# The last score packs of a head group's two sequences, run together in column tiles

## The chip, the cores and the metric

One Trainium2 chip, one core. The kernel computes two layers of a small model in float32. The metric is the time of one execution on the device, in microseconds (us). The changed kernel is run beside this one.

## The reference

Input x has 16 sequences of 256 tokens and 256 features. Each of the two layers is x + s * g on the normalised x, where s is a mixer and g a gate. The change touches the mixer of the second layer, an attention with 16 heads and latent keys:

```python
scores = jnp.einsum('bqhd,bkhd->bhqk', q, k) * scale
scores = jnp.where(mask, scores, jnp.finfo(scores.dtype).min)   # causal
attn = jax.nn.softmax(scores, axis=-1)
out = jnp.einsum('bhqk,bkhd->bqhd', attn, v).reshape(B, S, N_HEADS * V_DIM)
return out @ Wo
```

The first layer (a recurrence and a feed-forward gate) is not touched.

## The kernel before

**Tiling.** Tokens come in 8 chunks of two sequences (512 tokens). Heads come in groups of G = 4, so a chunk has four head groups, and there are 32 groups in all. One group of one sequence is a *unit*; there are 64, numbered i, and the main loop (`for i in range(LAST)`, L1649) spends one *slot* on each. Even slots hold sequence 0 of a group, odd slots sequence 1. Within a chunk the slot has a number r from 0 to 7; slot 31 is r = 7 of chunk 3, slot 34 r = 2 of chunk 4.

**Scores in blocks.** The 256 queries of a sequence are cut into NQ = 8 blocks of 32. Block a, with the four heads stacked, fills 128 rows and sees 32(a + 1) keys. `score_pack` (L1365) multiplies a few blocks into one PSUM bank: pack 0 has blocks 7 and 6, pack 1 has 5, 4 and 3, pack 2 has 2, 1 and 0 (96, 64 and 32 keys). For every block of a pack VectorE adds the mask (one instruction for the pack) and takes the row maximum; ScalarE takes the exponential, into the unit's buffer `pr`, with the row sums in `sr`. There are three PSUM banks for packs and two `pr` buffers, one for even and one for odd units.

**Column tiles.** A product can use the 128x128 array whole (128*128 in the profile) or half of its columns (128*64), so that two products with 64 rows of output stand side by side. Pack 2 of an even unit runs in two halves where it follows the products of values, which run in 64*64 tiles; this holds from slot 6 on. All other packs use the whole array.

**After the exponentials.** `normalise` (L1401) takes a reciprocal of the sums on VectorE and multiplies each block on GpSimd, one instruction for a block. Then three VectorE transposes (`turn`, L1414) write `turned`; the third, z = 0, reads blocks 0 to 3 and needs pack 2. `send` (L1426) stores it to DRAM (`far`) with four DMAs, and `fetch` (L1440) brings it back as `pT`, once for each half of the keys (y) and each sequence (b). `values_of` (L1486) multiplies `pT` by the values (`av`) for both sequences of a group, in the even slot four slots behind the group's first; it uses the half y = 0 first.

**Queries.** For a group two ahead, the odd slot multiplies queries (`pq`), rotates them on VectorE (`qmul`) and GpSimd (`qrot`, `query_rot`, L424); the next even slot begins with `query_move` (L430), eight DMAs that move `qrot` into `qg`.

**Order.** Every engine runs in the order written (`InOrder`), SyncE's DMA queue too: an instruction that waits holds up all behind it. SyncE's order is, in an even slot, query moves, fetch (y = 0, b = 0), the store of the odd unit before, fetch (y = 1, b = 0); in an odd slot, both fetches for b = 1, the store of the even unit before.

Before the change, an even slot's pack 2 comes after the values, then `normalise` of packs 0 and 1; an odd slot's pack 2 stands between the second and third query product, again followed by `normalise` of packs 0 and 1. Pack 2 of either unit is normalised in the slot behind, after that slot's pack 0.

**Other work in the slots.** At r = 6 the router of the next chunk (`router_chunk`, L318): products `pm`, then some twenty small VectorE instructions. At r = 7, in chunks 1 to 6, `fast_begin` (L1589): GpSimd multiplies and adds an output of the chunk before and stores it (`out_dram<-x`), between the normalising of the even unit's pack 2 and of the odd unit's packs 0 and 1. In the last chunk TensorE has output products instead of new queries.

Of the kernel before, what the change touches and what calls it, by code (L numbers as in the profile page):

```python
# [41 lines left out]
def tile_two_layers(ctx: ExitStack, tc: tile.TileContext, d: dict, out: bass.AP):  # L42
    nc = tc.nc

    class InOrder:


        def __init__(self, engine):
            self.engine, self.last = engine, None
# [151 lines left out]
    def bc(ap, n):  # L201

        return ap.unsqueeze(1).to_broadcast([ap.shape[0], n, ap.shape[1]])
# [226 lines left out]
    def query_move(n):  # L430
        q = groups[n]
        for r in range(2):
            for h in range(G):
                sp.dma_start(
                    q.qg[64 + 32 * r : 96 + 32 * r, :, h, :],
                    q.rot[32 * h : 32 * h + 32, r, :].rearrange("p (a q) -> p a q", q=32),
                )


    with ExitStack() as l0:  # L440
# [106 lines left out]
        def tiny(name, n=1):  # L547
            return w0.tile([P, n], F32, tag=name, name=name)
# [43 lines left out]
        u = tiny("u")  # L592
# [127 lines left out]
        def recur_mm(ch, xnT, ring):  # L720
            pb = ring.tile([P, S], F32, tag="mm", name=f"pb_{ch}")
            for c in range(2):
                for b in range(2):
                    pe.matmul(
                        pb[64 * b : 64 * b + 64, :], bT[:, c, :],
                        xnT[:, c, b * S : (b + 1) * S], start=(c == 0), stop=(c == 1),
                    )
            return pb

        def recur_in(ch, pb):  # L730

            v = a2.tile([P, S], F32, tag="v", name=f"v_{ch}")
            w = a2.tile([P, S], F32, tag="w", name=f"w_{ch}")
            v0.tensor_tensor(v, pb, ct, ALU.mult)
            swapped(w, pb)
            return v, w
# [519 lines left out]
        v, w = recur_in(ch, recur_mm(ch, xnT, ps_mm))  # L1256
# [73 lines left out]
    def gate_end(ch, jp):  # L1330
        k = chunks[ch]
        g = k.g2[:, 2 * jp : 2 * jp + 2, :]
        ve.scalar_tensor_tensor(g, g, 1.0, k.h, ALU.add, ALU.mult)
# [15 lines left out]
    for t in prs:  # L1349
        for a in range(NQ):  # L1350
            w = 32 * (a + 1)
# [3 lines left out]
    class Unit:  # L1355


        def __init__(self, i):
            self.i = i
            self.ch, r = divmod(i, 2 * NG)  # L1360
            self.g, self.b = divmod(r, 2)
            self.n = f"{self.ch}_{self.g}_{self.b}"
            self.pr = prs[i % NPR]

    def score_pack(u, pi):  # L1365
        k, b, pack = chunks[u.ch], u.b, PACK[pi]
        if pi == 0:
            u.nm = sm1.tile([P, NQ], F32, tag="nm", name=f"nm_{u.n}", bufs=3)
            u.sr = sm1.tile([P, NQ], F32, tag="sr", name=f"sr_{u.n}", bufs=3)
        qg = groups[u.i // 2].qg  # L1370
        sc = ps_sc.tile([P, CH], F32, tag="sc", name=f"sc_{u.n}_{pi}")
        halves = 2 if pi == 2 and u.b == 0 and u.i > 4 else 1
        m = P // halves
        for a, o in pack:
            w = qg[:, b * NQ + a, :, :].rearrange("p h q -> p (h q)")
            for y in range(halves):
                pe.matmul(
                    sc[m * y : m * y + m, o : o + 32 * (a + 1)], w[:, m * y : m * y + m],
                    k.kT[:, b * S : b * S + 32 * (a + 1)], start=True, stop=True,
                )  # L1380
        ends = [o + 32 * (a + 1) for a, o in pack]
        step = ends[1] - ends[0]
        n = len(pack)
        assert ends == [ends[0] + step * z for z in range(n)]
        if ends[0] - 32 + step * n <= CH:
            diag = sc[:, ends[0] - 32 : ends[0] - 32 + step * n].rearrange("p (n s) -> p n s", n=n)[:, :, 0:32]
        else:
            diag = sc[:, ends[0] - step : ends[-1]].rearrange("p (n s) -> p n s", n=n)[:, :, step - 32 : step]
        ve.tensor_tensor(diag, diag, bc(kmask, n), ALU.add)
        for a, o in pack:  # L1390
            ve.tensor_reduce(
                u.nm[:, a : a + 1], sc[:, o : o + 32 * (a + 1)], AX.X, ALU.max, negate=True
            )
        for a, o in pack:
            w = 32 * (a + 1)
            ac.activation(
                u.pr[:, OFF[a] : OFF[a] + w], sc[:, o : o + w], AF.Exp,
                bias=u.nm[:, a : a + 1], accum_out=u.sr[:, a : a + 1],
            )

    def normalise(u, packs):  # L1401
        blocks = [a for pi in packs for a, _ in PACK[pi]]
        lo, hi = min(blocks), max(blocks) + 1
        ve.reciprocal(u.sr[:, lo:hi], u.sr[:, lo:hi])
        for a in blocks:
            v = u.pr[:, OFF[a] : OFF[a] + 32 * (a + 1)]
            gp.tensor_scalar(v, v, u.sr[:, a : a + 1], 1.0, ALU.mult, ALU.mult)
# [32 lines left out]
    def fetch(n, y, b):  # L1440

        q = groups[n]
        if y == b == 0:
            q.pT = {}
        if b == 0:
            q.pT[y] = pp.tile([P, G, 3 * P], F32, tag="pT", name=f"pT_{n}_{y}", bufs=3)
        sp.dma_start(
            q.pT[y][64 * b : 64 * b + 64].rearrange("p h q -> p (h q)"),
            q.far[b].rearrange("(y k) s h z q -> y (k s) (h z q)", y=2)[y],
        )  # L1450
# [197 lines left out]
    units = [Unit(i) for i in range(LAST)]  # L1648
    for i in range(LAST):  # L1649
        ch, r = divmod(i, PER)  # L1650
        odd = i % 2 == 1
        u, w = units[i], units[i - 1] if i else None
        here = w is not None and w.i >= LAST - 2
        n = (i + 3) // 2 if odd else (i + 2) // 2
        n = n if n < len(groups) else None
        more = ch + 1 < NCH
        last = ch - 1 if ch == NCH - 1 and r in FINISH else None
        fast = ch - 1 if 0 < ch < NCH - 1 else None

        if not odd and n is not None:  # L1660
            query_move(n)
        if odd and i > 2:
            fetch((i - 3) // 2, 0, 1)
            fetch((i - 3) // 2, 1, 1)
        elif i and not odd:
            fetch((i - 2) // 2, 0, 0)
        score_pack(u, 0)
        if w:
            normalise(w, (2,))
        if fast is not None and r > 3:  # L1670
            fast_begin(fast, r)
        if ch > 1 and r == 0:
            fast_begin(ch - 2, 0)
        out_weights(i)
        if r == 1:
            gate_end(ch, 0)
        if r == 2:
            gate_end(ch, 1)
            if more and ch:
                norm_end(ch + 1)  # L1680
        if r == 5 and more:
            kv_end(ch + 1)
        if i == LAST - 1:

            finish_mm(last, 3, 0, NPAIR)
            finish_out(last, 3)
            last = None
        if w:
            for z in (1, 2):
                turn_here(w, z) if here else turn(w, z)  # L1690

        if r == 0:
            mid_chunk(ch)
        if r == 7 and more:
            key_chunk(ch + 1)
        if n is not None:
            query_mm(n, 0 if odd else 3)
            if not odd:
                query_lat(n, 3)
        if i == 5:  # L1700
            values_of(0)
        score_pack(u, 1)

        if odd and n is not None:
            query_mm(n, 1)
            query_mul(n, 0)
        if w:
            if here:
                turn_here(w, 0)
            else:  # L1710
                turn(w, 0)
                send(w)
        if not odd:
            if i > 4:
                values_of((i - 4) // 2)
            if i:
                fetch((i - 2) // 2, 1, 0)
        score_pack(u, 2)
        normalise(u, (0, 1))

        if odd and n is not None:
            query_mm(n, 2)
            query_mul(n, 1)
            query_rot(n)
            query_lat(n, 2)
        if r < 2:
            gate_begin(ch, r)
        if r == 0 and more and ch:
            norm_begin(ch + 1)
        if r == 2 and more:  # L1730
            transpose_chunk(ch + 1)
        if r == 4 and more:
            kv_begin(ch + 1)
        if r == 6 and more:
            router_chunk(ch + 1)
        if last is not None:
            j = FINISH.index(r)
            finish_mm(last, j, 0, NPAIR)
            finish_out(last, j)
        if fast is not None and r in FINISH:  # L1740
            fast_end(fast, r)
# [1 line left out]

    ch = NCH - 1
    u0, u1 = units[LAST - 2], units[LAST - 1]
    normalise(u1, (2,))

    finish_mm(ch, 0, 0, 4)
    finish_mm(ch, 1, 0, 4)
# [86 lines left out]
```

## Time and profile before

| | |
|---|---|
| median of 3 runs | 905.32 us (902.85 to 906.59) |
| profiled execution | 908.37 us, of it the span 906.6 us |
| granted TensorE clock, mean | 0.998 |
| second layer's slots | from about 272 us to the end |
| far<-turned, issue to landing, median | 4.3 us |
| pT<-far, issue to landing, median | 4.9 us |

A line of a timeline gives the start, the duration, the engine, the operation with output<-input, the shape, the count of instructions, and in brackets the idle time before it with what ended it. PE is TensorE, DVE VectorE, ACT ScalarE, POOL GpSimd, SPq SyncE's queue. A float32 product is recorded as two matmuls. L53 is the line of the helper that records the order, so groups are told apart by their tiles.

### The profile page before, as it was taken

Reading aid. Unit: us, or ns where it says so; the run is one execution under the profiler, and the core shown is the slowest. Engines: PE = TensorE matmul, PEld = TensorE weight load, DVE = VectorE, ACT = ScalarE, POOL = GpSimd, SP = SyncE. Lnnn points to the kernel's source line nnn. Section 1 sums busy time; section 2 is a strip of 40 time slices with the busy share of each in tenths; the row PEclk is TensorE's granted clock in tenths of the full one; section 3 lists DMA queues with packets and bytes.
Section 4 is the critical chain, followed back from the end, with each engine's and each line's share of the span. In section 5 each row is a group of like instructions: output and inputs, shape, how many; then the busy total and the mean of one; then the engine's idle time right before and its main releaser. Section 6 shows DMA issues by size and latency. Waiting matters only on the chain.

```text
span 906.6 us, 17800 instructions
## 1 busy us (share of the span) xinstructions
PE 893.3 (99%) x5600; PEld 668.2 (74%) x5600; DVE 666.4 (74%) x2017; ACT 476.1 (53%) x1562; POOL 571.5 (63%) x885
## 2 busy tenths in 40 slices
PE   8999999999999999999999999999999999999997
PEld 7768899888767656677677677667767766777775
DVE  6885687665586879768967876896786688687652
ACT  3334556564436656545554665565466556546451
POOL 1218787878345537687586768748776775876540
PEclk9999999999999999999999999999999999999999
DMA  9730000000013887877887888788788778968881
GB/s 283 236 108 10 1 2 1 1 1 1 1 24 71 195 218 190 217 175 176 212 212 175 211 197 181 177 224 202 175 212 186 198 172 213 221 163 206 198 230 38
DMA packets 197405, 134.02 MB, mean 148 GB/s; under 512 B 143104, under 2 KB 187968, under 8 KB 197312
## 3 DMA queue, kind: packets, MB, share of 16 engines
q1 hardware_dynamic: 195184, 128.69, 57.5%
q0 software_dynamic: 1152, 3.67, 1.3%
q8 instruction: 45, 0.74, 0.4%
q10 hardware_dynamic: 976, 0.53, 0.2%
q14 instruction: 48, 0.39, 0.1%
HBM read 63.11 MB, written 52.95 MB: 128 GB/s over the span
## 4 chain that ended last, share of the span: by engine, by line
PE 89%; DMA 4%; DVE 4%; POOL 1%; SPq 1%; issue 0%; ACT 0%; DVEq 0%; POOLq 0%; ACTq 0%
PE pq L53 21%; PE sc L53 13%; PE po L53 10%; PE av L53 8%; PE r L53 7%; PE f L53 7%; PE ph L53 5%; PE pf L53 5%; PE pg L53 4%; DMA far<-turned 2%; PE pm L53 2%; DMA pT<-far 2%; PE tp L53 2%; PE pkv L53 2%; PE py L53 1%; PE pb L53 1%
## 5 line engine op out<-in xcount | busy, mean ns | idle before, releaser
L53 POOL TENSOR_SCALAR pr<-pr,sr 128x256 f32<-128x256 f32 (+7 forms) x512 | 192.6, 395 | 186.4 <-DVE sr L53 177.6
L53 ACT ACTIVATE pr<-sc,nm 128x256 f32<-128x256 f32 (+7 forms) x512 | 190.2, 382 | 216.0 <-DVE sr L53 138.4
L53 PEld LDWEIGHTS sc<-kT,qg 128*128 128x128 f32 (+1 forms) x1198 | 150.0, 175 | 54.5 <-issue 41.2
L53 PE MATMUL sc<-kT,qg 128*128 128x32 f32 (+6 forms) x1198 | 167.8, 288 | 0.0
L53 DVE TENSOR_REDUCE nm<-sc 128x1 f32<-128x256 f32 (+7 forms) x512 | 127.7, 301 | 6.6
L53 DVE STREAM_TRANSPOSE turned<-pr 128x512 f32<-128x512 f32 x186 | 123.3, 688 | 11.1 <-POOL pr L53 10.9
L53 PE MATMUL pq<-xnT,wlat 128*128 128x512 f32 x256 | 122.6, 602 | 0.0
L53 PE MATMUL pq<-xnT,wrope 128*128 128x512 f32 x256 | 120.2, 593 | 0.0
L53 ACT ACTIVATION_READ_ACCUMULATOR pr<-sc,nm 128x1 f32 x512 | 104.0, 203 | 0.0
L53 PE MATMUL av<-pT,rowv 64*64 64x512 f32 (+2 forms) x992 | 82.4, 443 | 5.3 <-DMA pT<-far 5.3
L53 POOL TENSOR_TENSOR qrot<-qmul,qmul 128x512 f32<-128x512 f32 x64 | 83.6, 1326 | 2.8 <-DVE qmul L53 2.8
L53 DVE TENSOR_TENSOR sc<-sc,kmask 128x96 f32<-128x96 f32 (+1 forms) x192 | 45.5, 237 | 51.6 <-PE sc L53 50.2
L53 DVE TENSOR_TENSOR qmul<-pq,rot_q 128x512 f32<-128x512 f32 x128 | 80.9, 674 | 0.1
L53 ACT ACTIVATE qg<-pq 64x512 f32<-64x512 f32 x128 | 75.5, 590 | 4.3 <-PE pq L53 3.5
L53 PEld LDWEIGHTS av<-pT,rowv 64*64 64x64 f32 x992 | 40.3, 134 | 44.5 <-issue 25.3
L53 PEld LDWEIGHTS pq<-xnT,wrope 128*128 128x128 f32 x256 | 45.7, 191 | 32.4 <-issue 32.1
L53 PEld LDWEIGHTS pq<-xnT,wlat 128*128 128x128 f32 x256 | 45.7, 191 | 31.6 <-issue 31.6
L53 PEld LDWEIGHTS po<-wout,attT 128*128 128x128 f32 x416 | 58.4, 191 | 9.4 <-issue 4.0
L53 PE MATMUL po<-wout,attT 128*128 128x128 f32 (+1 forms) x416 | 64.2, 308 | 0.0
L53 POOL TENSOR_TENSOR rs<-ve,mhalf 128x4 f32<-128x4 f32 (+1 forms) x17 | 16.8, 987 | 48.0 <-DVE ve L53 33.0
L53 PE MATMUL ph<-xnT,p1T 128*128 128x256 f32 (+1 forms) x128 | 44.9, 508 | 0.8 <-DVE xnT L53 0.8
L53 POOL TENSOR_TENSOR attT<-attT,attT 128x512 f32<-128x512 f32 x36 | 45.1, 1272 | 0.0
(229 smaller groups left out, 1522.0 us busy)
## 6 DMA issues: line engine op xcount, KB each, us to landing
far<-turned SPq DMA_DIRECT2D x248, 192.0 KB, 4.3
pT<-far SPq DMA_DIRECT2D x124, 384.0 KB, 4.9
qg<-qrot SPq DMA_DIRECT2D x256, 64.0 KB, 2.5
x<-in_x_dram SPq DMA_DIRECT2D x7, 512.0 KB, 9.5
out_dram<-x POOLq DMA_DIRECT2D x12, 256.0 KB, 3.6
wqn_wo<-in_wq_nopeT_dram SPq DMA_DIRECT2D x4, 512.0 KB, 5.1
wqn_wo<-in_Wo_dram SPq DMA_DIRECT2D x4, 512.0 KB, 5.9
p2T<-in_proj2T_dram SPq DMA_DIRECT2D x2, 512.0 KB, 7.7
```

The source lines that it names most:

```text
L53: r = getattr(self.engine, name)(*args, **kw)
```

## The change

Pack 2 of both units of a group now runs in the even slot, one behind the other, always in two halves of 128*64, behind the products of values (in slots 0, 2 and 4, which have no values, behind pack 1). The odd slot has no pack 2 any more. The odd unit is normalised whole, eight blocks at once, at the place where packs 0 and 1 were; the slot behind an odd slot therefore has no `normalise` at its start. The even unit's `normalise` stays as it was: packs 0 and 1 in its own slot, behind both packs 2, and pack 2 in the odd slot behind.

```diff
     def score_pack(u, pi):
         k, b, pack = chunks[u.ch], u.b, PACK[pi]
-        if pi == 0:
+        if u.nm is None:
             u.nm = sm1.tile([P, NQ], F32, tag="nm", name=f"nm_{u.n}", bufs=3)
             u.sr = sm1.tile([P, NQ], F32, tag="sr", name=f"sr_{u.n}", bufs=3)
...
-        halves = 2 if pi == 2 and u.b == 0 and u.i > 4 else 1
+        halves = 2 if pi == 2 else 1
...
         score_pack(u, 0)
-        if w:
+        if odd:
             normalise(w, (2,))
...
-        score_pack(u, 2)
-        normalise(u, (0, 1))
+        if odd:
+            normalise(u, (0, 1, 2))
+        else:
+            score_pack(u, 2)
+            score_pack(units[i + 1], 2)
+            normalise(u, (0, 1))
...
     u0, u1 = units[LAST - 2], units[LAST - 1]
-    normalise(u1, (2,))
```

More of the change, by code (lines that the diff above doesn't have):

```diff
@@ L1363, in __init__ @@
             self.pr = prs[i % NPR]
+            self.nm = None
     def score_pack(u, pi):
         k, b, pack = chunks[u.ch], u.b, PACK[pi]
-        if pi == 0:
+        if u.nm is None:
             u.nm = sm1.tile([P, NQ], F32, tag="nm", name=f"nm_{u.n}", bufs=3)
```

## The prediction

> **What bounds the kernel now.** First the page: busy time by engine and the chain that ended last.
>
> ```profile
> PE 893.3 (99%) x5600; PEld 668.2 (74%) x5600; DVE 666.4 (74%) x2017; ACT 476.1 (53%) x1562; POOL 571.5 (63%) x885
> PE 89%; DMA 4%; DVE 4%; POOL 1%; SPq 1%; issue 0%; ACT 0%; DVEq 0%; POOLq 0%; ACTq 0%
> ```
>
> TensorE never rests. But a busy TensorE only says that other chains are not longer; one may be just as long. So next, TensorE's waits from 430 to 880 us:
>
> ```profile
> PE av L53 <- DMA pT<-far: 1.8, 2, 1.6
> ```
>
> The one thing it ever waits for is the transposed softmax coming back from DRAM. I follow that path once, from slot 30 (r = 6 of chunk 3) to slot 34. TensorE's timeline:
>
> ```profile
> 563.49 0.59 PE L53 MATMUL sc<-kT,qg 128*64 128x96 f32 x12
> 564.01 2.12 PE L53 MATMUL pm<-wmid,xnT 128*128 128x136 f32 x16
> ...
> 571.47 0.75 PE L53 MATMUL sc<-kT,qg 128*128 128x96 f32 x6
> 572.06 1.96 PE L53 MATMUL pq<-xnT,wlat 128*128 128x512 f32 x4
> ...
> 576.89 1.88 PE L53 MATMUL pq<-xnT,wlat 128*128 128x512 f32 x4
> ...
> 598.52 2.41 PE L53 MATMUL av<-pT,rowv 64*64 64x512 f32 x32
> ```
>
> VectorE waits for the router's products (pm), works through the router without a pause, and only then reaches slot 31's scores, 5.5 us late:
>
> ```profile
> 566.17 0.17 DVE L53 TENSOR_TENSOR lg<-pm,rb_bc 128x16 f32<-128x16 f32 x1 [0.75 <-PE pm L53]
> ...
> 571.45 0.23 DVE L53 TENSOR_TENSOR sc<-sc,kmask 128x64 f32<-128x64 f32 x1
> ...
> 572.35 0.17 DVE L53 RECIPROCAL sr<-sr 128x3 f32<-128x3 f32 x1
> ...
> 575.79 0.70 DVE L53 STREAM_TRANSPOSE turned<-pr 128x512 f32<-128x512 f32 x1
> ...
> 577.09 0.18 DVE L53 RECIPROCAL sr<-sr 128x5 f32<-128x5 f32 x1
> ```
>
> That reciprocal of 572.35 releases GpSimd, which then runs solidly up to the rotated queries (qrot):
>
> ```profile
> 572.68 0.91 POOL L53 TENSOR_SCALAR pr<-pr,sr 128x96 f32<-128x96 f32 x3 [5.32 <-DVE sr L53]
> ...
> 576.46 0.78 POOL L53 DMA_DIRECT2D out_dram<-x  x1 [0.30 <-POOL x L53]
> 577.38 2.03 POOL L53 TENSOR_SCALAR pr<-pr,sr 128x256 f32<-128x256 f32 x5
> 579.38 2.50 POOL L53 TENSOR_TENSOR qrot<-qmul,qmul 128x512 f32<-128x512 f32 x2
> 581.87 0.89 POOL L53 TENSOR_SCALAR pr<-pr,sr 128x96 f32<-128x96 f32 x3
> ```
>
> SyncE's queue stands at its eight query moves until the first qrot is done (idle 578.3 to 580.7), then issues without a pause of its own making (its only holds are landings of its own writes); the last two fetches follow in the second fence:
>
> ```profile
> 580.68 5.37 SPq L53 DMA_DIRECT2D qg<-qrot  x8
> 586.09 0.99 SPq L53 DMA_DIRECT2D pT<-far  x1
> 587.18 2.69 SPq L53 DMA_DIRECT2D far<-turned  x4
> 589.97 4.96 SPq L53 DMA_DIRECT2D pT<-far  x3
> ```
> ```profile
> L53 SPq DMA_DIRECT2D pT<-far x2: 451/520/588, 593.8 to 594.3; - x2
> DMA to landing us min/median/max: 4.4/4.9/5.5
> ```
>
> 594.3 + 5.5 = 599.8: the last block lands then. Slot 34's values begin at 598.52 and reach that block 1.34 us later, at 599.87. The slack is 0.05 us. So there are two bounds of equal length: TensorE, and the chain pm, router, reciprocal, GpSimd, qrot, SyncE, fetch. The same slack at the other chunk ends, landing against use: 443.1/442.7, 520.9/521.5, 678.3/678.2, 757.4/756.7, 835.9/835.8, that is -0.4, 0.7, 0, -0.7, -0.1. The groups between have up to 7 us, or hang on the same SyncE run as the one before.
>
> **The change, part by part.** (1) TensorE loses the odd slot's pack: 571.47 to 572.06, 0.59 us, once per group. (2) It gains a second tiled pack in the even slot. No row shows one alone. Above: 0.52 us (563.49 to 564.01), which includes entering and leaving the mode. Below: pure streaming; four pq instructions take 1.72 us in the timeline (576.89 to the next group at 578.61, a score pack), 0.84 ns per column, and a pack streams 2 x 192 columns with its two halves side by side, 0.32 us. I take 0.34, near the lower end, since the array is in the mode already. Net -0.25 per group for 29 groups, and about -0.2 for groups 0 to 2, whose first pack turns tiled as well, with a switch of mode (0.59 + 0.59 to 0.52 + 0.34, less about 0.1 for entering from the full array). Sum on TensorE: -7.9 us, were it the only bound.
>
> (3) Three normalisations move ahead of qrot on GpSimd. In slot 31 they stood behind it (581.87); start to next start, 0.86 us. What hides it? In slots with r = 1 and 3 SyncE is still busy when qrot ends (slot 33: ready at 597.4, issued at 598.4). At r = 5 the queue does wait, but the fetches it leads to have 5 us of slack. At r = 7 nothing hides it. The reciprocal now stands right behind the transpose that ends at 576.50, and slot 31's exponentials ended by 576.0, so it can come 0.6 us sooner; but GpSimd's store issue ends at 577.24, so normalising starts only 0.09 sooner. Chain: +0.86 - 0.09 = +0.77.
>
> (4) The second tiled pack stands ahead of pm: +0.34 in slot 30, and the router follows pm one for one. VectorE's four extra instructions there (0.7 us, by the first pack's) fit into its waits for pm (0.23 and 0.75). Chain from slot 30's start: +1.11.
>
> (5) ScalarE's three exponentials move with the pack; at 53% it has room, and slot 31's come after a 1.25 us gap anyway. The odd unit's even-slot transposes can start sooner, but its stores queue behind the query moves, so nothing arrives sooner. The probability buffer is free by then: the last transpose that reads it stands earlier on VectorE. One reciprocal per group (0.17 us) vanishes under other work.
>
> TensorE meanwhile comes to slot 34's values 0.34 - 0.59 + 0.34 - 0.59 = -0.49 earlier than before. It will wait about 1.11 + 0.49 - 0.05 = 1.55 us there. From values to values a chunk then changes by 1.11 - 0.49 = +0.62, less what slack there was.
>
> Sum: at the start of the layer, slot 1's qrot leads an unbroken SyncE run to the first waits. Slot 0 gains 0.36 us on TensorE, the reciprocal moves from 287.18 to 286.9, qrot +0.86: +0.58. Chunk 0's end (slot 7, no store there): the reciprocal now follows the transpose that ends at 340.88 instead of waiting until 341.47, so even with pm's +0.34 it comes 0.33 sooner; with the three operations, +0.53, on fetches that TensorE already waits for. Six chunk ends: 6 x 0.62 - 0.72 of positive slack = +3.0. After slot 55 SyncE runs unbroken to the last fetch, and TensorE already waits 1.8 us at 867 and 1.3 us at 885 for it, so later savings vanish and nothing comes back. Total +4.1 us: 908.37 to 912.5 for the profiled execution. That one ran 3.05 us over the median of the runs; carried over, 905.32 + 4.1 = 909.4 us.
>
> [...] The row: inside the tiled pack twelve weight loads fit into 0.52 us, switching included. [...]
>
> **Rivals.** *Faster: TensorE decides.* If fetches arrive early enough, parts 1 and 2 count in full: -7.9 us, 897.4; with half of the chunk ends hidden, about 902. For it: TensorE's 99%; and executions without profiling are 3 us shorter, perhaps in these very transfers. It decides where a chunk end has over 1.6 us of slack. Against it: the rows show 0.7 at most, five times of six none.
>
> *Slower still: the even unit gets late.* The even slot's reciprocal now stands behind the second pack on VectorE (0.7 us), so GpSimd's normalising, the next slot's transposes and the even unit's store follow later. If that store becomes what SyncE stands at, 0.7 us for seven chunks are added, +4.9: 914.3. It decides if the store is ready after the queue reaches it. Against it: slot 32's last transpose ends at 593.3 in slot 33 and the queue reaches its store at 595.0, so 1.7 us are spare.
>
> *The change doesn't do what it says: tiles run one by one.* Then the second pack costs 0.59, TensorE gains nothing, and pm comes 0.25 later in seven chunks: +1.8, 911.2.
>
> **How the numbers follow.** Forecast 0.60, faster 0.20, late even unit 0.13, tiles in turn 0.07. A measurement of this kernel can tell about 0.5%, 4.5 us, from no change, so 909.85 parts same from slower. The forecast's own range is 906.5 to 912.5 (0.15 us either way on seven steps, and each chain varies by some 0.4 us between chunks); two fifths of it are over the line. Slower: 0.24 + 0.13 + 0.06 = 0.43. Faster by over 0.5%: two thirds of its rival, 0.13. Same: 0.36 + 0.07 + 0.01 = 0.44. The range 901 to 914.5 leaves out the lower half of the faster rival and the upper half of the late one.
>
> **What would show it.** Right: TensorE's waits for pT between 430 and 880 grow several-fold, at the r = 2 slot behind each chunk end; eight normalisations stand in one GpSimd row of 2.9 us ahead of qrot; the two tiled packs take about 0.86 us together. Wrong: TensorE's waits stay under 2 us and chunks shorten by 1 us; or SyncE's idle time ends at far<-turned.

## The result, and the profile after

The changed kernel takes 916.27 us (median of 6 runs, 913.82 to 919.62) against 905.55 us (6 runs, 902.85 to 907.24). The ratio is 1.0116, 95% interval 1.009 to 1.0142. The forecast was 909.4, in a range of 901.0 to 914.5: the sign of the sum was right, its size was not. The profiled execution, the longest of the six, took 919.62 us, its span 917.8; what follows is read from it.

First the page and the chain that ended last, then TensorE's waits from 430 to 880 us:

```profile
PE 893.7 (97%) x5810; PEld 660.4 (72%) x5810; DVE 669.5 (73%) x1985; ACT 473.0 (52%) x1562; POOL 566.8 (62%) x885
PE 86%; DVE 7%; DMA 4%; ACT 1%; SPq 1%; issue 1%; POOL 0%; ACTq 0%; DVEq 0%; POOLq 0%
```
```profile
PE sc L53 <- ACT pr L53: 5.3, 5, 1.5
PE av L53 <- DMA pT<-far: 4.9, 5, 3.8
```

VectorE's share of the chain went from 4% to 7%. The second wait is the one I forecast. The first did not exist before: a score pack waits for ScalarE's exponentials. Of the waits that are listed it is the larger one inside the chunks; of the second, 3.8 us are one wait in the last chunk.

**The steps that came out.** TensorE around slots 30 and 31:

```profile
567.86 0.99 PE L53 MATMUL sc<-kT,qg 128*64 128x96 f32 x24
568.78 2.12 PE L53 MATMUL pm<-wmid,xnT 128*128 128x136 f32 x16
...
574.52 1.88 PE L53 MATMUL pq<-xnT,wrope 128*128 128x512 f32 x4
576.24 1.88 PE L53 MATMUL pq<-xnT,wlat 128*128 128x512 f32 x4
```

The two tiled packs take 0.92 us up to pm, where one took 0.52: the second costs 0.40 (0.34 was forecast). The odd slot's pack is gone; pq follows pq. VectorE, then GpSimd, then SyncE, as the chain was laid out:

```profile
570.94 0.17 DVE L53 TENSOR_TENSOR lg<-pm,rb_bc 128x16 f32<-128x16 f32 x1 [0.75 <-PE pm L53]
...
580.70 0.16 DVE L53 RECIPROCAL sr<-sr 128x8 f32<-128x8 f32 x1
```
```profile
580.75 0.78 POOL L53 DMA_DIRECT2D out_dram<-x  x1 [0.30 <-POOL x L53]
581.58 2.90 POOL L53 TENSOR_SCALAR pr<-pr,sr 128x256 f32<-128x256 f32 x8
584.45 2.51 POOL L53 TENSOR_TENSOR qrot<-qmul,qmul 128x512 f32<-128x512 f32 x2
```
```profile
585.75 5.60 SPq L53 DMA_DIRECT2D qg<-qrot  x8
```

Eight normalisations in one row of 2.90 us stand ahead of qrot, held back until the store is issued as worked out, and the query moves begin when the first qrot is done.

**The step that was not there.** Slot 34 (r = 2), GpSimd's qrot and VectorE before (one line and three), then VectorE and GpSimd's qrot after (five and one):

```profile
596.16 2.94 POOL L53 TENSOR_TENSOR qrot<-qmul,qmul 128x512 f32<-128x512 f32 x2
```
```profile
597.09 0.89 DVE L53 SCALAR_TENSOR_TENSOR g<-g,h 128x512 f32<-128x512 f32 x1
597.90 2.36 DVE L53 TENSOR_SCALAR xn<-x,mv,rs 128x256 f32<-128x256 f32 x4
...
601.40 0.23 DVE L53 TENSOR_TENSOR sc<-sc,kmask 128x96 f32<-128x96 f32 x1
```
```profile
600.83 3.04 DVE L53 SCALAR_TENSOR_TENSOR g<-g,h 128x512 f32<-128x512 f32 x1
603.79 1.37 DVE L53 TENSOR_SCALAR xn<-x,mv,rs 128x256 f32<-128x256 f32 x4
605.09 1.29 DVE L53 STREAM_TRANSPOSE turned<-pr 128x512 f32<-128x512 f32 x2
606.31 0.23 DVE L53 TENSOR_TENSOR sc<-sc,kmask 128x96 f32<-128x96 f32 x1
...
608.57 0.26 DVE L53 TENSOR_TENSOR sc<-sc,kmask 128x96 f32<-128x96 f32 x1
```
```profile
600.83 2.49 POOL L53 TENSOR_TENSOR qrot<-qmul,qmul 128x512 f32<-128x512 f32 x2
```

The gate product (g from g and h) takes 0.66 us in the median of its 16 instances before. Here it starts in the same moment as qrot and ends 0.55 us after it: 3.04 us. VectorE comes to pack 1's mask 7.40 us after the slot's first pack on TensorE (606.31 - 598.91) instead of 6.31 (601.40 - 595.09): 1.09 us late. TensorE then stands:

```profile
602.35 2.99 PE L53 MATMUL av<-pT,rowv 64*64 64x512 f32 x32
605.27 0.99 PE L53 MATMUL sc<-kT,qg 128*64 128x96 f32 x24
606.19 1.09 PE L53 MATMUL tp<-ident,xn 128*128 128x128 f32 x8
608.74 1.08 PE L53 MATMUL sc<-kT,qg 128*128 128x256 f32 x4 [1.46 <-ACT pr L53]
```

ScalarE's last exponential of pack 1 ends at 608.60. Why does a pack 0 wait for pack 1? The three banks are used in turn. Before, each slot had three packs, so pack 0 of an odd slot took the bank of pack 0 of the slot ahead. With four packs in the even slot it takes the bank of pack 1, which is freed 5.6 us later (in the trace of before 603.69 against 598.09).

The slots show it whole. These are mean lengths over chunks 2 to 6, from one slot's first pack to the next one's, worked out from the starts in the two timelines:

| slot r | 0 | 1 | 2 | 3 | 4 | 5 | 6 | 7 | chunk |
|---|---|---|---|---|---|---|---|---|---|
| before | 9.41 | 10.04 | 7.48 | 11.02 | 11.74 | 11.02 | 8.23 | 9.67 | 78.6 |
| after | 9.81 | 9.37 | 9.83 | 10.46 | 12.13 | 10.35 | 8.63 | 9.00 | 79.6 |

Three pairs of slots (r = 0 and 1, 4 and 5, 6 and 7) gain 0.27 us each, close to the 0.25 forecast, and slot r = 2 alone loses 2.35. In the best chunk before it takes 7.20 us; with 0.40 for the second pack its floor is 7.60, and 2.23 is lost above that.

Inside slot r = 2 this loss stands in two places, worked out from the starts as well. The values take 3.33 us on average, where they take 2.31 when no block of pT is late, and TensorE stands another 1.21 us ahead of the next slot's first pack. From chunk to chunk the two trade places (the values take 2.86 to 4.14 us), and yet the slot takes 9.83 to 9.85 us in all five. So the chain through VectorE and the bank sets its length, and the late fetches are hidden behind that chain.

By stretches of the two profiled executions: up to the end of chunk 0 -0.1, chunk 1 +2.2, chunks 2 to 6 +4.9, the last chunk, to the end of TensorE's last product, +4.4 (95.8 us instead of 91.5).

**The last chunk.** There values wait 3.8 us at once, and then TensorE runs at a granted clock of 0.50. The columns after the stretch are its length, busy time (and count) of PE, PEld, DVE, ACT and POOL, the granted clock, DMA share and GB/s:

```profile
876.00:880.00 4.00, 0.87 (x6) 0.54 (x10) 1.90 (x6) 1.24 (x6) 1.50 (x3) 0.78 0.91 232
880.00:884.00 4.00, 4.00 (x32) 1.84 (x26) 0.00 (x0) 0.68 (x2) 0.00 (x0) 0.50 0.46 171
884.00:888.00 4.00, 4.00 (x31) 3.51 (x28) 2.32 (x12) 2.28 (x13) 1.59 (x4) 0.50 0.87 260
888.00:892.00 4.00, 4.00 (x23) 3.53 (x22) 0.73 (x3) 1.18 (x5) 1.43 (x6) 0.94 0.91 226
```

The values' last block lands 62.0 us after the start of this chunk instead of 59.2. Slot 55's query moves begin 0.9 us later after the chunk's start, as its qrot ends later, and take 6.7 us instead of 5.4, so the fetch behind them is issued 2.3 us late. Half of that is gone again at the fetch after it (1.2), and the two groups of query moves behind that one, 7.1 and 7.5 us instead of 6.3 each, bring it to 2.6 at the last fetch. Why the moves take longer is open.

### The profile page after: what moved, and what is told of

It is laid out like the page before. It is cut to its first block, busy times and chain, and to the rows that moved or that the text cites. A ratio compares the mean times of both kernels' runs of the same rounds, so it can differ in the third digit from the quotient of the medians.

```text
span 917.8 us, 18157 instructions
## 1 busy us (share of the span) xinstructions
PE 893.7 (97%) x5810; PEld 660.4 (72%) x5810; DVE 669.5 (73%) x1985; ACT 473.0 (52%) x1562; POOL 566.8 (62%) x885
## 4 chain that ended last, share of the span: by engine, by line
PE 86%; DVE 7%; DMA 4%; ACT 1%; SPq 1%; issue 1%; POOL 0%; ACTq 0%; DVEq 0%; POOLq 0%
PE pq L53 20%; PE sc L53 12%; PE po L53 11%; PE r L53 7%; PE f L53 7%; PE av L53 6%; PE ph L53 5%; PE pf L53 5%; PE pg L53 4%; DVE g L53 2%; DMA pT<-far 2%; DMA far<-turned 2%; PE pm L53 2%; PE pkv L53 2%; ACT pr L53 1%; DVE nm L53 1%
## 5 line engine op out<-in xcount | busy, mean ns | idle before, releaser
L53 POOL TENSOR_SCALAR pr<-pr,sr 128x256 f32<-128x256 f32 (+7 forms) x512 | 190.6, 395 | 196.1 <-DVE sr L53 178.4
L53 PEld LDWEIGHTS sc<-kT,qg 128*64 128x64 f32 (+1 forms) x1408 | 137.0, 163 | 51.8 <-issue 33.1
L53 PE MATMUL sc<-kT,qg 128*64 128x96 f32 (+7 forms) x1408 | 158.8, 278 | 9.0 <-ACT pr L53 8.8
L53 PE MATMUL pq<-xnT,wlat 128*128 128x512 f32 x256 | 120.2, 592 | 0.0
L53 ACT ACTIVATION_READ_ACCUMULATOR pr<-sc,nm 128x1 f32 x512 | 108.1, 211 | 0.0
L53 DVE TENSOR_TENSOR sc<-sc,kmask 128x64 f32<-128x64 f32 (+1 forms) x192 | 46.5, 242 | 69.5 <-PE sc L53 68.3
L53 PE MATMUL av<-pT,rowv 64*64 64x512 f32 (+2 forms) x992 | 86.9, 446 | 6.9 <-DMA pT<-far 6.8
L53 POOL TENSOR_TENSOR qrot<-qmul,qmul 128x512 f32<-128x512 f32 x64 | 80.9, 1286 | 2.8 <-DVE qmul L53 2.8
L53 PEld LDWEIGHTS pq<-xnT,wlat 128*128 128x128 f32 x256 | 48.0, 190 | 46.0 <-issue 45.9
```

Source lines behind the costliest of these rows:

```text
L53: r = getattr(self.engine, name)(*args, **kw)
```

## The experiments

Several theories were set against each other: **A**, the shorter reuse of banks and the late VectorE add up; **B** or **D**, one of them alone, or nothing but TensorE once they are gone; **C**, my prediction's own chain of qrot, query moves and fetches. Ratios are to the kernel before on the same chip, with 95% intervals; it took 906.42 to 909.32 us on the chips used here, so times expected in us are to be read with the ratio beside them. Chunk lengths are means over chunks 2 to 6 of the profiled execution. Part of TensorE's waiting stands between the single products of values, where it is not listed as a wait, so lengths of slot r = 2 are compared, and inside it the stretch of the values (waits for fetches) and the stand at its end (waits for exponentials).

### e1: the odd unit's pack 2 normalised in the slot behind again

```diff
-        if odd:
+        if w:
             normalise(w, (2,))
...
-            normalise(u, (0, 1, 2))
+            normalise(u, (0, 1))
...
+    normalise(u1, (2,))
```


> The changed kernel, with the odd unit's pack 2 normalised where it was before, in the slot behind, so that the rotated queries (qrot) start after five normalisations again. Packs and column tiles stay as changed. In the profile of the changed kernel, slot r = 2 takes 9.83 us instead of 7.20, and TensorE's new wait there is for ScalarE's exponentials of pack 1. Theory A (banks and late VectorE, half and half): of the 2.23 us that this slot lost beyond the tiled pack, about 1.09 come from VectorE being held until qrot ends and 1.14 from the shorter reuse of the three banks. Then the chunk goes from 79.58 to about 78.5 us, TensorE still waits about 1.1 us per chunk for pack 1's exponentials, and the time is 906 to 908 us. Theory B (late VectorE is all of it): no wait for the exponentials, chunk 77.4 to 77.8, time 899 to 903. Theory C (the query moves and fetches, as predicted): waits for pT of about 0.8 us per chunk instead, chunk 78.2, about 904.

Measured: 907.65 us where the kernel before ran 909.32 on this chip, ratio 0.9985 (0.9971 to 0.9999). The chunk takes 78.5 and slot r = 2 8.76. So undoing the reordering gives back 1.07 us of the 2.23 in each chunk, and 1.16 stay. That is A's size but not A's split: of the 1.16, 0.74 stand in the values, so they are the fetches, and 0.42 at the slot's end, where A put about 1.1. In slot 34 qrot starts at 595.16, after five normalisations, and the gate product takes 0.85 us again.

### e2: the reordering alone

```diff
-        if w:
+        if odd:
             normalise(w, (2,))
...
             query_mul(n, 1)
+        if odd:
+            normalise(u, (2,))
+        if odd and n is not None:
             query_rot(n)
...
-    normalise(u1, (2,))
```


> The kernel before with one part of the change alone: the odd unit's pack 2 is normalised in its own slot, just ahead of qrot, as three more operations there; packs, column tiles and bank order stay as before. Theory A: qrot is 0.86 us later and holds VectorE as in the changed kernel, but TensorE's first pack of slot r = 3 needs only the bank of pack 0, so no wait for exponentials appears; what remains is the wait for pT, about 0.8 us at each of seven chunk ends: 909 to 911 us. Theory B: late VectorE alone costs what the changed kernel lost: waits for the exponentials of about 1 us per chunk, 912 to 915. Theory C: 0.8 us per chunk end in waits for pT, 910.

Measured: 914.15 us where the kernel before ran 909.32 on this chip, ratio 1.0042 (1.0022 to 1.0062). VectorE is held as in the changed kernel (the gate product takes 3.06 us in slot 34), and yet there is no wait for exponentials from 430 us on. Slot r = 2 goes from 7.48 to 7.68, the last chunk from 91.5 to 93.1, the first two from 146.3 to 150.9. B falls: with three packs in every slot a late VectorE costs TensorE almost nothing there. What the late qrot costs by itself stands mostly at the two ends of the layer, in the profiled execution at least, which is the longest of twelve (916.64).

### e3 and e3b: both packs 2 in one bank

```diff
+        if pi == 2:
+            if u.b == 0:
+                u.bank = ps_sc.tile([P, CH], F32, tag="sc", name=f"sc_{u.n}_{pi}")
+            sc = units[u.i - u.b].bank[:, S * u.b : S * u.b + S]
+        else:
+            sc = ps_sc.tile([P, CH], F32, tag="sc", name=f"sc_{u.n}_{pi}")
```


> The changed kernel, with both packs 2 of a group in one PSUM bank (columns 0 to 223 and 256 to 479), so that a group takes five banks and the first pack of an odd slot again reuses the bank of pack 0 of the slot ahead. All else as changed. Theory A: the waits for pack 1's exponentials (8.8 us in all) vanish; the fetches then decide, as predicted: waits for pT of up to 1.5 us per chunk, chunk 78.9, time about 909 to 911. Theory B: VectorE stays late, and TensorE still waits for exponentials: 913 to 916. Theory C: the banks are beside the point, the chunk stays at 79.5 us, 914 to 916.

Measured: 1029.72 us, ratio 1.1324 (1.1289 to 1.1358), and the question was not answered. From 430 to 840 us:

```profile
PE sc L53 <- ACT pr L53: 48.5, 17, 5.4
```

In every even slot the second pack's products waited for the exponentials of the first, about 3 us. e3b therefore multiplies both packs first (`score_mm`) and masks them afterwards (`score_post`).

```diff
+    def score_last(u, v):
+        sc = ps_sc.tile([P, CH], F32, tag="sc", name=f"sc_{u.n}_2")
+        args = [score_mm(x, 2, sc[:, S * x.b : S * x.b + S]) for x in (u, v)]
+        for a in args:
+            score_post(a)
...
-            score_pack(u, 2)
-            score_pack(units[i + 1], 2)
+            score_last(u, units[i + 1])
```


> The changed kernel, with both packs 2 of a group in one PSUM bank, and now with the products of both packs ahead of the masks and exponentials of either. In the first try each second pack waited about 3 us for the exponentials of the first (94 us of waits in 32 slots). The first pack of an odd slot again reuses the bank of pack 0 of the slot ahead. Times are relative to the kernel before on the same chip. Theory A (banks and late VectorE add up): no waits for exponentials are left, and the late fetches decide instead, so waits for pT of about 1.5 us stand at the chunk ends: chunk 78.6 to 79.0, ratio 1.002 to 1.006. Theory B (late VectorE alone): TensorE still waits for exponentials, chunk 79.5, ratio 1.011. Theory D (banks alone): no wait grows elsewhere, chunk 77.4, ratio 0.99.

Measured: 915.66 us, ratio 1.0087 (1.0053 to 1.0121); the profiled execution, 912.84, was the shortest of six. TensorE's waits from 430 to 840 us:

```profile
PE av L53 <- DMA pT<-far: 2.0, 4, 1.1
PE pq L53 <- DVE qmul L53: 1.0, 5, 0.2
```

No wait for exponentials is left although the eight normalisations still stand ahead of qrot: the wait came through the banks. Slot r = 2 takes 8.95, and the 1.35 above its floor, all in the values, are now the fetches, near the 1.55 of the prediction. Slot r = 0 loses 0.44, since VectorE's mask of the second pack now waits 1.90 us for the first one's exponentials in the same bank, and query products come late. So the chunk is 79.1, the upper edge of what A allowed, and the time is over it.

### e4b: one bank, and the normalising back

The edits of e3b and e1 together.

> As the run before, and the odd unit's pack 2 is normalised in the slot behind again, so that qrot starts as early as in the kernel before. What is left of the change is the two tiled packs one behind the other (0.25 us less for TensorE in a group) and 0.34 to 0.40 us more ahead of the router's products. Theory A: neither the banks nor VectorE hold TensorE; the fetches come 0.4 us later against values that come 0.5 sooner, so about 0.8 us of waits for pT at each chunk end: chunk 78.1 to 78.3, ratio 0.995 to 0.998. Theory D: the chunk goes to 77.4 whichever place the normalising has, ratio 0.99.

Measured: 910.20 us, ratio 1.0020 (0.9998 to 1.0042), chunk 78.7. Slot r = 2 takes 8.48: with neither banks nor qrot in the way, 0.88 above the floor is left, which A put at 0.8 and D at nothing. The rest of the miss is the same 0.44 in slot r = 0.

### e5: the gate product behind pack 1

```diff
-        if r == 2:
-            gate_end(ch, 1)
-            if more and ch:
-                norm_end(ch + 1)
...
         score_pack(u, 1)
+        if r == 2:
+            gate_end(ch, 1)
+            if more and ch:
+                norm_end(ch + 1)
```


> The changed kernel, with one step moved: in slot r = 2 VectorE's gate product (g from g and h) and the normalising of the next chunk's x come behind pack 1 instead of behind pack 0, so that they no longer stand ahead of the transposes and pack 1 while qrot runs. Theory A: pack 1's exponentials end about 2 us sooner after the start of the slot, the wait for them falls from about 1.3 us per chunk to under 0.3, and the waits for pT grow to up to 1.5: chunk about 79.0, time 909 to 912. Theory B: chunk 77.5 to 78, time 900 to 905. Theory C: nothing changes, 914 to 916. If the step is now late for the transposes of x (tp), TensorE waits for VectorE's xn there.

Measured: 911.10 us, ratio 1.0020 (1.0002 to 1.0038). Banks and qrot are as in the changed kernel; only what VectorE has ahead of pack 1 changed. The one wait from 430 to 840 us:

```profile
PE av L53 <- DMA pT<-far: 0.4, 1, 0.4
```

Slot r = 2 takes 8.41 and the chunk 78.1, shorter than A's 79.0: the waits for pT did not grow to 1.5, but to 0.8. The gain is lost at the ends (the first two chunks take 150.1 us and the last 93.7, against 146.3 and 91.5 before), where waits of 3.8 and 2.4 us are each followed by stretches at a granted clock of 0.50.

### e6 and e7: qrot ahead of the normalising

```diff
-            normalise(u, (0, 1, 2))
+            pass
...
             query_rot(n)
+        if odd:
+            normalise(u, (0, 1, 2))
+        if odd and n is not None:
```


> The changed kernel, with the odd unit's eight normalisations behind qrot in their own slot instead of ahead of it. qrot can then start when its inputs are there (about 1.8 us sooner in slots 31 and 33), and the queue's query moves with it; the three banks are used as in the changed kernel. Theory A: VectorE's gate product and x's normalising are held 1.8 us less, but the next transposes wait for normalisations that end 2.5 us later; so pack 1's exponentials end about 1 us sooner, and 1.1 us of waits for them remain per chunk, while the waits for pT at the chunk ends vanish: chunk 78.4, ratio 0.997 to 1.000. Theory B: chunk 77.4 to 77.8, ratio 0.99. Theory C (query moves and fetches): all of the loss goes, and TensorE's saving counts: ratio 0.990 to 0.993.

Measured: 911.37 us, ratio 1.0044 (1.0026 to 1.0062), chunk 79.0. The waits for pT between 430 and 870 us vanish entirely (the values take 2.31 us in each of the five chunks), and yet TensorE waits 1.21 us per chunk for exponentials. So C alone falls: the bank wait is there without any late fetch. A's chunk was 0.6 too short; slots r = 0 and 1 take 0.45 more than in the changed kernel, and why is open.

> Both: eight normalisations behind qrot, and both packs 2 in one bank with their products first. Theory A: neither wait is left inside the layer, so TensorE's saving of 0.25 us per group counts nearly whole: chunk 77.4 to 77.7, ratio 0.988 to 0.992, unless the odd unit's transposes, which now wait for later normalisations, bring a new wait. Theory C: as the run before.

Measured: 930.22 us, ratio 1.0246 (1.0217 to 1.0275), a miss. GpSimd's sums for the fast output products are now late, and TensorE waits for them (`po` for `attT`, 5.0 us in ten waits) and for the normalised x (`tp` for `xn`, 1.1 us in three).

### e11 and e10: a store moved out of the chain

GpSimd's product, sum and store of slot r = 7 go to slot r = 1 behind, in the changed kernel (e11) and in e9 (e10). The product's buffer moves with them.

```diff
-        if fast is not None and r > 3:
+        if fast is not None and 3 < r < 7:
             fast_begin(fast, r)
...
+        if ch > 1 and r == 1:
+            fast_begin(ch - 2, 7)
...
-            k.c1 = a2.tile([P, 2, D], F32, tag="h", name=f"c1_{ch}", bufs=1)
+            k.c1 = k.attT[1][:, 1, :].rearrange("p (j n) -> p j n", j=2)
```

> The changed kernel, with one step taken out of the chain ahead of qrot at the chunk ends: in slot r = 7 GpSimd's product, sum and store of an output of the chunk before (3.7 us) move to slot r = 1 behind. The eight normalisations of slot 31 then start when their reciprocal is there, 0.7 us sooner, and qrot, query moves and fetches with them. Banks and slots r = 2 stay as changed. Theory A (banks and late VectorE set the chunk): the waits for pT go, those for pack 1's exponentials grow by as much, the chunk stays at 79.5 us, ratio 1.009 to 1.012. Theory C (the fetches set it): chunk 78.9, ratio 1.005.

> As e9, and GpSimd's product, sum and store of slot r = 7 move to slot r = 1 behind. The reciprocal in slot r = 7, which stands right behind a transpose now, then releases the normalising 0.6 us sooner than before the change, against 0.4 lost ahead of the router: the chain to the fetches is 0.2 us shorter than in the kernel before. Theories A and C alike: chunk 77.5 to 77.8, ratio 0.989 to 0.993. If GpSimd's three instructions are in the way in slot 33 instead (they have 4.1 us of idle time there before the change), qrot of that slot is late and nothing is won.

Measured: e11 947.54 us, ratio 1.0453 (1.0429 to 1.0477); e10 918.91 us, ratio 1.0137 (1.0111 to 1.0164). Both miss, for a reason of my own making. That product reads the gate of an earlier chunk, and there are two buffers for gates. So slot 32's new gate on ScalarE now waits for GpSimd's product in slot 33 (e11; in e10 the same wait is 5.62 us):

```profile
608.29 0.63 ACT L53 ACTIVATE g<-h 128x512 f32<-128x512 f32 x1 [5.60 <-POOL attT L53]
```

VectorE, and qrot after it, are later still in slot 34. The chain at r = 7 is shorter, there are no waits for pT, and the chunk is 85.3: what happens in slots r = 1 and 2 sets it. The wait ahead of slot 35 grows to 2.7 us, and TensorE's granted clock falls (first TensorE's line, then the stretches after it):

```profile
624.27 1.97 PE L53 MATMUL sc<-kT,qg 128*128 128x256 f32 x4 [2.69 <-DVE nm L53]
```
```profile
624.20:627.20 3.00, 2.93 (x6) 2.15 (x7) 1.69 (x10) 3.00 (x16) 2.04 (x5) 0.50 0.73 131
627.20:630.20 3.00, 3.00 (x6) 1.44 (x6) 1.33 (x4) 1.63 (x6) 0.90 (x3) 0.50 1.03 319
630.20:633.20 3.00, 3.00 (x11) 1.68 (x10) 2.23 (x7) 1.15 (x6) 0.00 (x0) 0.97 0.80 207
```

In the 3.2 us ahead of 624.2 TensorE was busy for only 0.58, so the listed 2.69 is not all of its idle time.

### e9: normalising back and gate product behind pack 1

The edits of e1 and e5 together; banks as changed.

> The changed kernel with two steps undone or moved: the odd unit's pack 2 is normalised in the slot behind, as before the change, and in slot r = 2 VectorE's gate product and x's normalising come behind pack 1. Theory A: no waits for exponentials; the fetches decide, later by 0.4 us (the second tiled pack ahead of the router) against values that come 0.5 sooner: chunk 78.2, ratio 0.996 to 0.998. Theory D (TensorE decides as soon as banks and VectorE are out of the way): chunk 77.4, ratio 0.990.

Measured: 902.40 us, ratio 0.9958 (0.9937 to 0.9980): faster than the kernel before, where the changed one was slower. The chunk takes 77.8, between A's 78.2 and D's 77.4, and slot r = 2 8.14. From 430 us on there is no wait for exponentials; the 0.54 above the floor stand in the values, so they are the fetches.

### e8: as e9, with the odd pack 2 of r = 6 left in its own slot

```diff
+            if r == 7 and more:
+                score_pack(u, 2)
...
-            score_pack(units[i + 1], 2)
+            if r < 6 or not more:
+                score_pack(units[i + 1], 2)
```


> As e9, and in slots r = 6 with a router the odd unit's pack 2 stays in the odd slot as before, so that the router's products come no later than in the kernel before. Three groups of four have the joint packs. The chain from the router to the fetches is that of the kernel before: of TensorE's 0.75 us per chunk, the 0.5 between the values and the router's products count, and 0.2 turn into waits for pT: chunk 77.9, ratio 0.993 to 0.996 (theories A and C alike). Theory D: 77.6.

Measured: 900.94 us, ratio 0.9960 (0.9937 to 0.9983), chunk 77.9 as expected. Against e9 it is the same within the intervals: slots r = 6 and 7 lose 0.27 (17.90 against 17.63) and slot r = 2 gains 0.17 (7.97 against 8.14).

### e14: the moved gate product alone

e5's edit in the kernel before.

> The kernel before, with one step moved: in slot r = 2 VectorE's gate product and the normalising of the next x come behind pack 1. No joint packs. Theory A: the kernel before has no wait for exponentials at TensorE, so nothing is gained: chunk 78.3 to 78.6, ratio 0.998 to 1.001, and the gain of the run with both comes from the joint packs once VectorE no longer stands behind qrot. Theory E (the moved step is the gain): ratio 0.995 to 0.997.

Measured: 907.76 us, ratio 1.0013 (0.9996 to 1.0030), chunk 78.65. The moved step alone gains nothing. E falls, and e9's gain needs the joint packs.

### e13 and e12: the store where GpSimd is idle

In slot r = 7 the same three instructions come ahead of the even unit's normalising, in the changed kernel (e13) and in e9 (e12, where the condition is `w`).

```diff
+        if fast is not None and r == 7:
+            fast_begin(fast, r)
         if odd:
             normalise(w, (2,))
-        if fast is not None and r > 3:
+        if fast is not None and 3 < r < 7:
             fast_begin(fast, r)
```

> The changed kernel, with GpSimd's product, sum and store of slot r = 7 ahead of the even unit's three normalisations there instead of behind them; GpSimd is idle for 4.7 us at that place, and the three take 3.7. The eight normalisations then start when their reciprocal is there, 0.7 us sooner. Theory A (banks and late VectorE set the chunk): chunk stays at 79.5, ratio 1.009 to 1.012. Theory C (fetches set it): chunk 78.9, ratio 1.005. A risk: GpSimd's product and sum (1.27 us each) now run beside the router's small VectorE instructions, and if these are held as the gate product was, the chain gets up to 2.5 us longer instead: then waits for pT of 2 us and more at the chunk ends and a ratio over 1.015.

> As e9 (normalisation of the odd unit's pack 2 in the slot behind, gate product behind pack 1), with the same move of GpSimd's product, sum and store in slot r = 7. Theory A and C alike: the chain to the fetches gets 0.6 us shorter, chunk 77.4 to 77.6, ratio 0.991 to 0.994. If VectorE's router is held by GpSimd's product and sum, the chain gets up to 2.5 us longer: ratio 1.00 to 1.01.

Measured: e13 926.60 us, ratio 1.0219 (1.0197 to 1.0241); e12 909.98 us, ratio 1.0039 (1.0022 to 1.0056). The risk named came true: VectorE's small instructions are held. VectorE's router in e13, then GpSimd:

```profile
576.00 1.14 DVE L53 SCALAR_TENSOR_TENSOR l<-oh,lg 128x32 f32<-128x32 f32 x1
577.18 0.19 DVE L53 TENSOR_REDUCE m<-l 128x4 f32<-128x32 f32 x1
577.40 1.09 DVE L53 TENSOR_TENSOR eq<-l,m 128x32 f32<-128x32 f32 x1
```
```profile
575.79 1.30 POOL L53 TENSOR_TENSOR c<-c,g 128x512 f32<-128x512 f32 x1
577.17 1.26 POOL L53 TENSOR_TENSOR x<-x,c 128x512 f32<-128x512 f32 x1
```

Here the GpSimd product and sum each hold one small VectorE instruction (1.14 and 1.09 us, 0.19 each in the changed kernel) until they end: 1.85 us more in the chain. The loss does not show as the waits for pT that were expected. In e13 slot r = 2 stays at 9.82, and slots r = 7 and 0 lengthen to 9.37 and 10.67 us, where TensorE waits for `kT` and `qmul`. So whether that chain, shortened cleanly, would move the changed kernel was not settled.

## Why the prediction was wrong

**Right:** parts (1) and (2) in their sum, a gain of 0.27 us for 0.25 in each pair of slots without a wait, though both terms were low (the pack taken out was worth 0.67 for 0.59, the second one cost 0.40 for 0.34) and the two errors cancel; that entering from the full array costs about 0.1 (pack 1 takes 0.91 us up to the values, 320.54 to 321.45 before, and 0.82 up to a query product, 282.44 to 283.26); of part (3), qrot behind eight normalisations and the query moves behind qrot; and that TensorE's 7.9 us would not arrive. The fetches' price was roughly right too: forecast 1.55 us of waiting per chunk, measured 1.35 where the banks were taken out of the way (e3b). The sign of the sum came out right in part by this and in part for a reason that the prediction did not have.

**The step that failed** is in part (3), "What hides it?", and in (5). I asked only who waits for qrot in SyncE's queue, and wrote the delay off at r = 1, since the queue is busy there. But qrot of that slot runs on into slot r = 2, and there it is not SyncE but VectorE that pays: 3.04 us for an instruction of 0.66. The trace of before had the sign of it: beside qrot the gate product took 0.89 there and x's normalising 2.36, where the changed kernel's, behind qrot, takes 1.37. I did not read it. The second half is a part that is missing: the change moves a pack from one slot to another, and I did not count through the three banks, so pack 0's new dependence on pack 1 went unnoticed, under the words "ScalarE has room". The two are links of one chain, not halves of a sum as theory A had it: with either taken away (e3b, e5) no wait for exponentials is left from 430 us on. With both, slot r = 2 lost 2.23 us above its floor where the fetches alone would have taken 1.35 to 1.55; these do not add, the latest one counts. Relieving qrot leaves 1.16 (e1), VectorE's order 0.81 (e5), both together 0.54 (e9). For chunks 1 to 6 the sum said +2.9 (0.53, and five chunk ends of 0.62 less 0.72 of slack), and the traces say +7.0.

**A second term, mis-sized:** "after slot 55 SyncE runs unbroken to the last fetch ... later savings vanish and nothing comes back" was right as a path, but the sum gave the last chunk no more than the 0.62 of its own slot r = 2, and it took 4.4 us: that slot lost 1.9 and slot r = 6 5.1, and others gained. The late qrot of slot 55 starts that path 0.9 us later, and query moves that take longer bring the delay to 2.6; why they do is open. The wait at the end of the path grew to 3.8 us, and TensorE's granted clock stood at 0.50 for some 9 us after it.

**The rivals:** "TensorE decides" did not occur. The even unit's store was not what SyncE stood at: in slot 33 the last transpose for it ends at 597.8, and the queue reaches it at 599.4. Tiles do run side by side: the second pack's 0.40 us holds twelve loads and their products, where the full pack taken out was worth 0.67.

## What to carry to other kernels

When an instruction moves to another slot, count through every ring of buffers it takes part in: a fourth pack in a slot shifted which exponential a later, untouched pack waits for. When an engine is delayed, ask not only who waits for its result but what runs beside it during the delay; here GpSimd held VectorE (3.04 us for an instruction of 0.66), so the delay surfaced in an instruction that depends on neither. And test a gain with each new wait removed by itself: the packs gave 0.4% against the kernel before only after two steps around them had been put back or moved (e9; e14 has the moved step without the packs and gains nothing).

## What the runs showed of the hardware

**VectorE held by GpSimd.** The gate product took 3.04 us beside two qrot (2.49 us) and 0.66 without; the router's instructions 1.14 and 1.09 beside one GpSimd instruction each (e13), and 0.19 without. In the same stretch of e13 a reduction (m from l, 0.19) was not held. In slot 34 of the changed kernel VectorE was held through both qrot, one directly behind the other. It is not always so. In slot 34 before, the gate product began during the first qrot and ended 0.55 us after that one, and the second qrot took 1.71 us instead of 1.27. What decides between the two cases no run here shows, but three normalisations moved ahead of qrot, and nothing else, lengthened this instruction in slot 34 from 0.89 to 3.06 us (e2).

**The clock after a wait.** After the 3.8 us wait in the changed kernel, and after each of the waits of 2.7 us in e11's chunks 2 to 6, TensorE's granted clock stood at 0.50 for 6 us or more; after a wait of 3.5 us in e9 it did so for 3 us, and after the waits of 1.4 to 1.5 us in the changed kernel's r = 2 slots it stayed at 1.00. Between 1.5 and 2.5 us both happened: in the changed kernel it stayed at 1.00 after waits of 1.73 and 2.06 us (325.70 and 369.98), in the kernel before it stood at 0.50 for 3 us after one of 1.98 (324.51). The listed wait does not tell all: in e11 TensorE had little work around its waits too (0.58 us in the 3.2 ahead of slot 35). What a wait near 2 us can cost beside its own length is an estimate from the clocks of such stretches: 1.5 us in the kernel before (3 us at 0.50), and 3.4 after one of e14's waits of 1.9 us (9 us at 0.63, 0.50 and 0.74). Whether that makes the wide spread of some runs (e3b, 912.84 to 919.23), no run here shows.
